# Local score stores moved from SP's DMA queue to ACT's, with a new order of phases

## The chip, the cores and the metric

The kernel runs on one core of a Trainium2 chip. The metric is the device time of one execution in microseconds. The core has a matrix engine (PE, with its weight loads shown as PEld), a vector engine (DVE), a scalar engine (ACT), a third elementwise engine (POOL) and a queue engine (SP) that here does nothing but begin DMAs. [...] DMAs are begun by SP and by ACT.

## The reference

The input is x of 8 sequences, 1024 positions, 256 channels, float32. Three residual layers follow each other:

```python
x = x + 0.5 * ffn(layernorm(x))
x = x + attn(layernorm(x))
x = x + 0.5 * ffn(layernorm(x))
```

`ffn` mixes each row with the row before it (`mu * x + (1 - mu) * x_prev`, once for k and once for r) and gives `sigmoid(xr @ W_r.T) * (relu(xk @ W_k.T)**2 @ W_v.T)`. `attn` has 16 heads of 16 channels, and looks at 40 fixed distances instead of all positions: 0 to 32, and 48, 64, 96, 128, 192, 256, 384.

```python
for i, o in enumerate(OFFSETS):
    qk = jnp.einsum('bhnd,bhnd->bhn', q, _shift(k, o))
    lg = qk * inv * (1.0 + qs[..., i]) + pos_bias[i][None, :, None]
p = jax.nn.softmax(jnp.stack(logits, axis=-1), axis=-1)
out = sum(p[..., i][..., None] * _shift(v, o))
```

Here `qs` is the product of q with a small table per distance. The result is scaled by head, multiplied by a sigmoid gate of x, and projected.

## The kernel before

Positions are handled in 32 chunks of 256 (4 a sequence) and, in the attention, in 64 tiles of 128. Groups of 512 positions (i, 16 of them, four tiles each) share the projected q. The work is written as generators, and each `yield` ends a phase:

- `ffn(c, "a")` and `ffn(c, "b")` (L230): the two FFNs of a chunk, called f1 and f2 in the plan. Normalisation: stats on DVE (L207), a chain of eight small POOL operations (L212 to L219), two scalings xn on ACT (L224), transposes on PE (L226). Then the mixing on ACT and DVE (L241, L246), three matrix products (p, L195), relu, square, tanh on ACT, the residual add on POOL (L280).
- `project(c)` (L286), p in the plan: the same normalisation, then q, k, gate and v; q to the tile qst (L311), k spread to kst (L317), v to the tile vn and from there to a DRAM buffer vd (L351).
- `scores` (L356): products of q with k for 32 rows at a time into two PSUM tiles, and two ACT copies (L370). It is called by `far` (L376) and `local` (L400).
- `local(tt)`: the scores of a tile against its own neighbourhood, copied by ACT into the SBUF tile sl (two buffers) and written by four DMAs into a DRAM buffer sl_d. A skewed address in the later read turns the band into columns by distance. `far` does the same for the long distances with sf.
- `attend(tt)` (L417): loads the logits lg from sl_d and sf_d (L425, L429); loads v (vw and v3, L435 to L446); the small product gp (L454) and its use (L458); the bias on POOL (L461); maximum and subtraction on DVE (L464, L465); exp on ACT (L467) and right behind it, on ACT's own DMA queue, the store of the near probabilities to DRAM (pd<-lg, L468); products with v for the long distances on POOL and DVE; the load of the skewed probabilities back (pd<-pd, L497); transposes (tra, L514), copies ptt on ACT (L520), products with v (pv, L527); division on DVE; on every second tile the output product (L561) and the residual add (L563).

The order is set by hand. Every phase of every generator has a place in the tables PLAN and WARP: a number of chunks, to which the chunk's or half the tile's number is added. All phases are sorted by place and emitted in that order, and every engine's queue follows it. A place is no time. With the step of one chunk the same pattern returns, with variants for even and odd tiles and for `far`, which comes twice in the first group of a sequence half and four times in the second. WARP shifts the first four and the last ten chunks.

In the program as built, the DMAs of SP and ACT together are given eight semaphores in turn. A DMA whose semaphore is still held by an earlier one waits for that one's landing, on the engine that begins it.

Of the kernel before, what the change touches and what calls it, by code (L numbers as in the profile page):

```python
# [42 lines left out]


PLAN = {
    "setup": (94.301, 95.430, 96.861),
    "f1": (-6.891, -5.181, -4.113, -3.628, -3.556, -3.503, -3.223, -3.134, -3.030, -2.933, -2.814, -2.771),
    "p": (-2.636, -2.595, -2.382, -2.366, -2.209, -2.155, -2.084, -1.868, -1.644, -1.528, -1.432),
    "f2": (1.626, 1.748, 1.930, 2.004, 2.060, 2.208, 2.297, 2.414, 2.553, 2.580, 2.713, 4.437),
    "far": (  # L50
        (-0.987, -0.918),
        (-0.874, -0.608),
        (-0.990, -0.939),
        (-0.777, -0.772),
        (-0.751, -0.627),
        (-0.528, -0.523),
    ),
    "loc": (
        (-1.515, -1.348),
        (-0.848, -0.610),  # L60
        (-1.298, -1.048),
        (-1.496, -1.489),
    ),
    "att": (
        (-0.277, -0.025, -0.020, 0.011, 0.092, 0.296, 0.358, 0.413, 0.416, 0.471, 0.743, 0.779, 0.784, 0.838, 0.892, 0.971, 1.094, 13.222),
        (-0.404, 0.000, 0.016, 0.041, 0.111, 0.194, 0.295, 0.315, 0.427, 0.447, 0.621, 0.660, 0.673, 0.723, 0.824, 0.884, 0.938, 1.093),
    ),
}
WARP = {
    ("att", 0): 0.012, ("att", 1): 0.014, ("att", 2): 0.002, ("att", 3): -0.006, ("att", 22): 0.010, ("att", 23): 0.002, ("att", 24): -0.008, ("att", 25): 0.032, ("att", 26): 0.048, ("att", 27): 0.036, ("att", 28): 0.026, ("att", 29): -0.049, ("att", 30): -0.064, ("att", 31): -0.076,  # L70
    ("f1", 0): -1.203, ("f1", 1): -0.910, ("f1", 2): -0.739, ("f1", 3): 0.153, ("f1", 22): 0.006, ("f1", 23): 0.025, ("f1", 24): -0.009, ("f1", 25): -0.004, ("f1", 26): 0.009, ("f1", 27): 0.026, ("f1", 28): 0.017, ("f1", 29): 0.027, ("f1", 30): 0.045, ("f1", 31): 0.053,
    ("f2", 0): 0.006, ("f2", 1): 0.006, ("f2", 2): -0.013, ("f2", 3): 0.001, ("f2", 22): 0.006, ("f2", 23): -0.003, ("f2", 24): 0.043, ("f2", 25): 0.041, ("f2", 26): 0.025, ("f2", 27): 0.477, ("f2", 28): 0.422, ("f2", 29): 0.543, ("f2", 30): 0.373, ("f2", 31): 0.119,
    ("far", 0): -0.275, ("far", 2): -0.001, ("far", 22): 0.004, ("far", 24): 0.035, ("far", 26): 0.044, ("far", 28): 0.047, ("far", 30): -0.024,
    ("loc", 0): -0.699, ("loc", 1): -0.010, ("loc", 2): 0.023, ("loc", 3): 0.047, ("loc", 22): 0.037, ("loc", 23): 0.007, ("loc", 24): 0.043, ("loc", 25): 0.074, ("loc", 26): 0.045, ("loc", 27): 0.056, ("loc", 28): 0.007, ("loc", 29): 0.037, ("loc", 30): 0.014, ("loc", 31): 0.120,
    ("p", 0): -0.906, ("p", 1): -0.868, ("p", 2): -0.096, ("p", 3): 0.024, ("p", 22): -0.017, ("p", 23): -0.005, ("p", 24): 0.014, ("p", 25): 0.005, ("p", 26): -0.008, ("p", 27): -0.040, ("p", 28): 0.034, ("p", 29): 0.045, ("p", 30): 0.006, ("p", 31): -0.018,
}


def flat(t, off, *dims):
    return bass.AP(tensor=t.tensor, offset=off, ap=[list(d) for d in dims])  # L80
# [3 lines left out]
def macaron(ctx: ExitStack, tc: tile.TileContext, x, wffn, watt, wo, cols, rows, pbias, se, mask, out):  # L84
    nc = tc.nc
# [270 lines left out]
    def scores(o, i, q4, keys):  # L356


        p = [ps.tile([128, 512], F32, name="p", tag=f"psq{r}", bufs=2) for r in range(2)]
        for g in range(2):  # L360
            for s in range(len(q4(0))):
                for a in range(4):
                    ms = q4(a)[s]
                    for r in range(2):
                        rows = slice(64 * r, 64 * r + 64)
                        kk = ks[g][rows, keys(ms)].rearrange("n j (h q) -> n j h q", h=2)
                        pp = p[r][32 * a : 32 * a + 32].rearrange("n (j h g q) -> n j h g q", h=2, g=2, q=2)
                        mm(pp[:, s * 32 : s * 32 + kk.shape[1], :, g], qs[i][rows, g, ms], kk, True, True)
        for r in range(2):
            nc.scalar.mul(  # L370
                o.rearrange("n j h g q -> n (j h g) q")[:, :, 2 * r : 2 * r + 2],
                p[r].rearrange("n (m q) -> n m q", q=2),
                WS**-2,
            )
# [25 lines left out]
    def local(tt):  # L400
        i, t = tt // 4, tt % 4
        sl = psb.tile([128, 64, 2, 2, 4], F32, name="sl")
        scores(
            sl,
            i,
            lambda a: [slice(t * 128 + 32 * a, t * 128 + 32 * a + 32)],
            lambda ms: slice(512 * (i % 2) + ms.start, 512 * (i % 2) + ms.start + 64),
        )
        yield
        for a in range(4):  # L410
            nc.sync.dma_start(
                flat(sl_d[i % 2], (4 * t + a) * BLK, (ROW, 32), (1, ROW)),
                sl[32 * a : 32 * a + 32].rearrange("n j h g q -> n (j h g q)"),
            )
        yield
# [165 lines left out]
    for tt in range(B * NT):  # L581
        add("loc", tt / 2, local(tt), PLAN["loc"][tt % 4])
        add("att", tt / 2, attend(tt), PLAN["att"][tt % 2])
# [66 lines left out]
```

## Time and profile before

| what | value |
|---|---|
| median of 3 runs | 1022.88 us (1022.44 to 1028.41) |
| profiled execution | 1026.83 us, of which the span from first to last instruction 1024.8 us |
| mean granted PE clock | 0.971 |
| ACT, largest groups | xn L224 104.9 us; xm L241 100.4; ptt L520 74.7; sl L370 72.7; sf L370 55.0 |
| idle time of ACT ahead of xh L291, gt L329 | 58.7 and 56.0 us, ended by PE |
| DMA | 208.75 MB, mean 204 GB/s, engines about 70% to 80% busy in the middle |
| issues by SP of sl<-sl | 256 of 128 KB, median 3.4 us to landing |
| issues by ACT of pd<-lg | 64 of 264 KB, median 2.8 us to landing |
| SP's waits for pd<-lg ahead of L497 | 203.2 us in 61 waits |

How to read it: busy time of an engine does not count instructions that only begin DMAs, nor waits. "L195 p<-kst,qst" is PE at line 195 writing p from kst and qst; a matrix product of float32 operands appears as two records. "A <- B" in the waits means that A's engine stood idle until B ended. In the timelines the columns are the start, the time, the engine (SPq, ACTq: a queue's issue of a DMA), line, operation, tiles, and in brackets the idle time before it.

### The profile page before, as it was taken

The numbers are of one execution on the slowest core, as the hardware profiler recorded it, in microseconds if no ns is written. First come the engines' busy times: TensorE is split into PE (matmuls) and PEld (weight loads), VectorE is DVE, ScalarE is ACT, GpSimd is POOL, SyncE is SP. The second block draws the span as 40 slices with busy tenths as digits, with TensorE's granted clock in tenths as the row PEclk, the third lists the DMA queues.
The fourth block names the chain that finished last, engine by engine and source line by source line (L and its number), as shares of the span: only waits on it lengthen the run. The fifth ranks groups of instructions, "written<-read, shape, count | busy, mean of one in ns | idle before, by whom it ended". The sixth has DMA issues, their size and how long they took to land.

```text
span 1024.8 us, 36078 instructions
## 1 busy us (share of the span) xinstructions
PE 951.4 (93%) x14592; PEld 781.3 (76%) x14592; DVE 831.9 (81%) x1670; ACT 610.4 (60%) x1218; POOL 695.5 (68%) x1240
## 2 busy tenths in 40 slices
PE   3888899999999999999999999999999999976775
PEld 2666688888888888888888888888888888854554
DVE  4446889988999789888999789988999789866761
ACT  3454666676666766676666766676666766543332
POOL 5434778767877688667787678767886778543641
PEclk9899999999999999999999999999999999988888
DMA  8257777768777776777877777688776777757530
GB/s 241 62 157 204 221 227 200 222 200 249 214 219 216 215 237 198 214 228 218 236 207 225 220 237 211 196 236 244 222 212 210 205 227 216 211 161 234 166 110 21
DMA packets 204365, 208.75 MB, mean 204 GB/s; under 512 B 77288, under 2 KB 162472, under 8 KB 204200
## 3 DMA queue, kind: packets, MB, share of 16 engines
q1 hardware_dynamic: 194984, 189.16, 64.8%
q10 hardware_dynamic: 9216, 17.31, 4.6%
q8 instruction: 114, 1.87, 0.8%
q14 instruction: 51, 0.42, 0.1%
HBM read 110.26 MB, written 96.14 MB: 201 GB/s over the span
## 4 chain that ended last, share of the span: by engine, by line
PE 81%; DMA 4%; POOL 4%; DVE 4%; issue 3%; ACT 2%; SPq 1%; ACTq 0%; POOLq 0%; DVEq 0%
PE p L195 55%; PE pv L195 6%; PE tra L195 5%; PE tra L514 5%; PE tr L226 5%; PE gp L195 4%; PE tra L547 1%; DMA lg<-sl 1%; ACT xn L224 1%; POOL y L213 1%; POOL x L280 1%; DMA sf<-sf 1%; DVE prod L505 1%; DMA pd<-pd 1%; DVE st L207 1%
## 5 line engine op out<-in xcount | busy, mean ns | idle before, releaser
L195 PE MATMUL p<-w_f,xm 128*128 128x256 f32 x1024 | 251.3, 389 | 0.0
L195 PEld LDWEIGHTS p<-w_f,xm 128*128 128x128 f32 x1024 | 187.5, 192 | 42.2 <-issue 12.7
L461 POOL TENSOR_TENSOR lg<-lg,bias 128x640 f32<-128x640 f32 x64 | 99.0, 1547 | 85.8 <-DVE lg L458 74.6
L195 PE MATMUL p<-xm,w_f 128*128 128x256 f32 x512 | 128.6, 396 | 8.4 <-DVE xm L248 5.2
L224 ACT ACTIVATE xn<-x,nb,y 128x256 f32<-128x256 f32 x192 | 104.9, 599 | 32.4 <-POOL nb L219 16.4
L241 ACT ACTIVATE xm<-tr,col 128x256 f32<-128x256 f32 x256 | 100.4, 475 | 39.8 <-PE tr L226 33.9
L195 PE MATMUL p<-kst,qst 64*32 64x256 f32 (+1 forms) x4096 | 123.6, 362 | 0.5 <-DVE kst L317 0.3
L246 DVE SCALAR_TENSOR_TENSOR xm<-tr,rest,xm 128x255 f32<-128x255 f32 x256 | 105.5, 474 | 21.2 <-ACT xm L241 19.9
L195 PEld LDWEIGHTS p<-xm,w_f 128*128 128x128 f32 x512 | 96.5, 198 | 25.6 <-issue 10.4
L508 POOL TENSOR_TENSOR far<-prod 128x272 f32<-128x272 f32 x64 | 49.0, 765 | 93.3 <-DVE prod L505 86.2
L280 POOL TENSOR_TENSOR x<-x,xm 128x512 f32<-128x512 f32 x64 | 81.9, 1279 | 39.9 <-DVE xm L278 39.9
L195 PE MATMUL p<-xh,wa_hi 128*128 128x256 f16 x384 | 105.1, 274 | 0.0
L195 PE MATMUL p<-xh,wa_lo 128*128 128x256 f16 x384 | 104.9, 273 | 0.0
L195 PE MATMUL p<-xl,wa_hi 128*128 128x256 f16 x384 | 104.9, 273 | 0.0
L482 POOL TENSOR_TENSOR prod<-vn,lg 128x272 f32<-128x272 f32 x144 | 94.9, 671 | 14.2 <-ACT lg L467 12.8
L520 ACT COPY ptt<-tra 128x512 f32<-128x512 f32 x128 | 74.7, 584 | 43.7 <-PE tra L514 27.8
L226 PE MATMUL tr<-ident,xn 128*128 128x128 f32 x384 | 66.4, 293 | 33.2 <-ACT xn L224 32.7
L505 DVE TENSOR_TENSOR prod<-prod 128x544 f32<-128x544 f32 (+2 forms) x120 | 93.6, 780 | 3.6
L195 PEld LDWEIGHTS pv<-vw,ptt 128*32 128x32 f32 x4096 | 69.2, 157 | 33.3 <-ACT ptt L520 17.3
L195 PEld LDWEIGHTS p<-kst,qst 64*32 64x32 f32 x4096 | 75.7, 122 | 22.9 <-issue 10.7
L317 DVE SCALAR_TENSOR_TENSOR kst<-p,col,kown 128x1024 f32<-128x1024 f32 x64 | 78.7, 1271 | 13.5 <-PE p L195 13.5
L514 PE MATMUL tra<-ident,pd 128*128 128x128 f32 x512 | 80.1, 280 | 10.3 <-DMA pd<-pd 6.7
(79 smaller groups left out, 2051.5 us busy)
## 6 DMA issues: line engine op xcount, KB each, us to landing
sl<-sl SPq DMA_DIRECT2D x256, 128.0 KB, 3.4
pd<-pd SPq DMA_DIRECT2D x64, 512.0 KB, 4.3
sf<-sf SPq DMA_DIRECT2D x184, 128.0 KB, 3.2
vw<-vd SPq DMA_DIRECT2D x128, 136.0 KB, 4.1
v<-vd SPq DMA_DIRECT2D x64, 272.0 KB, 4.4
lg<-sl SPq DMA_DIRECT2D x64, 264.0 KB, 3.9
pd<-lg ACTq DMA_DIRECT2D x64, 264.0 KB, 2.8
vd<-vn SPq DMA_DIRECT2D x32, 272.0 KB, 4.8
```

Source lines behind the costliest of these rows:

```text
L195: nc.tensor.matmul(o, l, r, start=start, stop=stop)
L224: nc.scalar.activation(xn, x2[:, i], AF.Identity, bias=nb[:, i : i + 1], scale=y[:, i : i + 1])
L226: nc.tensor.transpose(tr[:, c, i * 128 : i * 128 + 128], xn[:, c * 128 : c * 128 + 128], ident)
L241: nc.scalar.activation(xm[:, o, h], tr[:, h], AF.Identity, scale=mu[:, h : h + 1])
L246: nc.vector.scalar_tensor_tensor(x_[:, 1:256], tr[:, h, 0:255], m, x_[:, 1:256], ALU.mult, ALU.add)
L280: nc.gpsimd.tensor_tensor(x2, x2, xr, ALU.add)
L317: nc.vector.scalar_tensor_tensor(ks[g][:, o : o + 256], p[:, g].unsqueeze(2).to_broadcast([128, 256, 4]), b_k[:, g : g + 1], kown.unsqueez ...
L461: nc.gpsimd.tensor_tensor(la, la, bias[:, min(t, 3)].rearrange("p u e -> p (u e)"), ALU.add)
L482: nc.gpsimd.tensor_tensor(prod[:, k], shifted[k][1](), lf[:, k].unsqueeze(2).to_broadcast([128, 16, 17]), ALU.mult,)
L505: nc.vector.tensor_tensor(terms[:, 0:m], terms[:, 0:m], terms[:, n - m : n], ALU.add)
L514: nc.tensor.transpose(tr[:, pr * 128 : pr * 128 + 128], pd.rearrange("p (m e) -> p m e", e=8)[:, :, 4 * g + pr], ident,)
L520: nc.scalar.copy(ptt.rearrange("p q n -> p (q n)"), tr)
```

## The change

Two edits. The first is in `local`: the `yield` between the copies and the stores goes, so that both are one phase, and ACT begins the four stores instead of SP. Line numbers from there on fall by one (L468 becomes L467, L497 becomes L496).

The second is a new plan: all places in PLAN and WARP have other numbers. Most of the steady pattern keeps its order on each engine, with small moves. The lines that matter here:

```diff
 PLAN = {
...
-    "p": (-2.636, -2.595, -2.382, -2.366, -2.209, -2.155, -2.084, -1.868, -1.644, -1.528, -1.432),
+    "p": (-2.546, -2.486, -2.309, -2.298, -2.183, -2.139, -2.042, -1.760, -1.580, -1.487, -0.264,),
...
     "loc": (
-        (-1.515, -1.348),
-        (-0.848, -0.610),
-        (-1.298, -1.048),
-        (-1.496, -1.489),
+        (-1.451,),
+        (-0.919,),
+        (-1.267,),
+        (-1.435,),
     ),
     "att": (
-        (-0.277, -0.025, -0.020, 0.011, 0.092, 0.296, 0.358, 0.413, 0.416, 0.471, 0.743, 0.779, 0.784, 0.838, 0.892, 0.971, 1.094, 13.222),
-        (-0.404, 0.000, 0.016, 0.041, 0.111, 0.194, 0.295, 0.315, 0.427, 0.447, 0.621, 0.660, 0.673, 0.723, 0.824, 0.884, 0.938, 1.093),
+        (-0.069, 0.034, 0.038, 0.061, 0.197, 0.297, 0.376, 0.466, 0.481, 0.483, 0.541, 0.619, 0.797, 0.877, 0.956, 1.010, 1.189, 14.063,),
+        (-0.518, -0.024, 0.059, 0.074, 0.108, 0.255, 0.313, 0.442, 0.499, 0.501, 0.708, 0.757, 0.786, 0.836, 0.908, 0.996, 1.042, 1.175,),
     ),
 }
 WARP = {
...
-    ("f2", 0): 0.006, ("f2", 1): 0.006, ("f2", 2): -0.013, ("f2", 3): 0.001, ("f2", 22): 0.006, ("f2", 23): -0.003, ("f2", 24): 0.043, ("f2", 25): 0.041, ("f2", 26): 0.025, ("f2", 27): 0.477, ("f2", 28): 0.422, ("f2", 29): 0.543, ("f2", 30): 0.373, ("f2", 31): 0.119,
+    ("f2", 0): -0.004, ("f2", 1): -0.012, ("f2", 2): -0.026, ("f2", 3): -0.009, ("f2", 22): -0.024, ("f2", 23): -0.012, ("f2", 24): -0.009, ("f2", 25): -0.018, ("f2", 26): -0.029, ("f2", 27): 0.619, ("f2", 28): 0.412, ("f2", 29): 0.219, ("f2", 30): 0.050, ("f2", 31): 3.965,
...
 }
...
@@ def local(tt) @@
             lambda a: [slice(t * 128 + 32 * a, t * 128 + 32 * a + 32)],
             lambda ms: slice(512 * (i % 2) + ms.start, 512 * (i % 2) + ms.start + 64),
         )
-        yield
         for a in range(4):
-            nc.sync.dma_start(
+            nc.scalar.dma_start(
                 flat(sl_d[i % 2], (4 * t + a) * BLK, (ROW, 32), (1, ROW)),
                 sl[32 * a : 32 * a + 32].rearrange("n j h g q -> n (j h g q)"),
             )
```

In the order that follows from it, the steady state differs on SP and ACT more than on PE. The four stores of sl stand on ACT between the copies of a tile and whatever ACT does next. On SP the loads of vw and v3 for an odd tile now stand just ahead of the even tile's pd load, instead of behind it; the store of vd of a chunk is issued more than a chunk later; the two tiles' lg loads stand closer together. At the end, the second FFN of chunk 30 (its products, L262 to L276) comes ahead of the output product of the last tile, and the first products of that of chunk 29 ahead of the last tile's maximum. At the start, the stats of chunks 1 and 2 and the POOL chain of chunk 1 come ahead of the clearing of buffers.

## The prediction

> **What bounds the kernel now.** I read the page first, then the table of stretches, the waits, the chain that ended last, and last the timelines of single engines. The page:
>
> ```profile
> PE 951.4 (93%) x14592; PEld 781.3 (76%) x14592; DVE 831.9 (81%) x1670; ACT 610.4 (60%) x1218; POOL 695.5 (68%) x1240
> ...
> PE   3888899999999999999999999999999999976775
> ```
>
> PE is the bound, and not evenly. In the table of stretches (columns: stretch, its length, busy time of PE, PEld, DVE, ACT and POOL, granted clock, DMA share, GB/s):
>
> ```profile
> 25.00:50.00 25.00, 19.87 (x141) 14.97 (x142) 11.25 (x30) 11.25 (x23) 12.56 (x28) 0.82 0.20 56
> 500.00:600.00 100.00, 100.00 (x1676) 83.81 (x1676) 89.17 (x179) 66.19 (x135) 74.69 (x132) 1.00 0.77 220
> 925.00:950.00 25.00, 15.53 (x275) 11.23 (x281) 13.01 (x25) 8.90 (x17) 11.66 (x18) 0.77 0.76 229
> ```
>
> From 100 to 900 us PE is busy 793.9 of 800, at full clock. The other 67 us of its idle time lie before 100 (28) and after 900 (39). So in the middle, 78% of the span, a new plan has 6 us to win; whatever delays PE there is lost one for one.
>
> What can delay it? The waits name ACT; the third line is a wait of ACT for a *load that SP began*:
>
> ```profile
> PE tr L226 <- ACT xn L224: 32.7, 9, 8.9
> PE pv L195 <- ACT ptt L520: 12.6, 9, 4.0
> ACT ptt L520 <- DMA lg<-sl: 4.4, 3, 2.4
> ```
>
> A ptt copy (L520) reads no such load. The chain of waits and the timelines of ACT and PE show what happens, at 406 to 415 us:
>
> ```profile
> 406.19 7.00 DMA lg<-sl
> ```
> ```profile
> 410.53 0.74 ACT L467 ACTIVATE lg<-lg 128x640 f32<-128x640 f32 x1
> 413.27 0.33 ACTq L468 DMA_DIRECT2D pd<-lg  x1
> 413.63 0.58 ACT L520 COPY ptt<-tra 128x512 f32<-128x512 f32 x1 [2.37 <-PE p L195]
> ```
> ```profile
> 414.27 1.21 PE L195 MATMUL pv<-vw,ptt 128*32 128x34 f32 x64 [1.02 <-ACT ptt L520]
> ```
>
> The exp ends at 411.27; the store behind it, the one DMA that ACT begins now, starts at 413.27, 0.08 after that load landed at 413.19. In the built program the DMAs of SP and ACT share eight semaphores in turn, so DMA n waits until DMA n-8 has landed, whichever queue began it. Of ACT's 64 stores 15 start late in the trace, 16.2 us in all, the longest 4.40 at 927.5, each 0.07 or 0.08 us after the landing of the DMA eight before, where that is recorded. ACT's next instructions stand behind. Of four PE gaps over 1 us between 100 and 900 (2.36, 1.10, 1.02 and 1.08), the 1.10 (at 125.6) and the 1.02 follow such a late store.
>
> **The change, part by part.**
>
> *Removed from SP:* 256 stores of sl at about 0.44 us (four in 1.76 us), 113 us of its queue. SP's long wait is L497 for the landing of pd<-lg, 203 us in 61 waits, which stays. The loads that were queued behind sl may start up to 1.8 us sooner; the middle has nothing to win by it. Value 0; between -6 and 0.
>
> *Added to ACT:* 256 issues. The row is pd<-lg on ACT's queue: 0.326 us each, about 0.37 from start to start; 85 to 95 us, 1.5 a tile. ACT is 65% busy in the middle, so the cover is its slack. Behind each group of four stand: for tiles t=0 and t=1 (t is the tile's number modulo 4) the two xn of a projection, whose transposes PE runs next; for t=2 a relu and a ptt; for t=3 the gate's tanh and a ptt. Two copies end 1.3 after the last score product, four issues end at 3.0, xn at 3.6; PE has 4.4 us of other work in front of the transpose for t=0 (gp, four second-layer products, the output product) and 3.8 for t=1 (no gp). For t=2 the ptt ends at 4.2 and is due at 5.1, for t=3 the tanh's input comes only at 3.5. (Due times: mean starts of PE's matmuls in the trace of before, summed over the changed order.) Covered, by 0.2 us at the thinnest: cost 0, were nothing waited for.
>
> *The wait that is added:* each of these 256 also waits for its DMA n-8. In the changed program about 190 of them look at SP's queue. For t=0 (12 of 16 tiles) they are, in order, a v load, the pd load, an lg<-sl load, an lg<-sf load; for t=1 the pd load and a vd store are among the four; for t=2 mostly ACT's own stores, long landed; for t=3 a pd store, the pd load, two vw loads. The pd load cannot begin before the pd store has landed, and that store is ACT's own, 12 to 15 of ACT's instructions earlier. So ACT waits for a round trip that it started itself. The pieces:
>
> ```profile
> pd<-pd SPq DMA_DIRECT2D x64, 512.0 KB, 4.3
> ...
> lg<-sl SPq DMA_DIRECT2D x64, 264.0 KB, 3.9
> ...
> vd<-vn SPq DMA_DIRECT2D x32, 272.0 KB, 4.8
> ```
> ```profile
> 599.10 0.33 ACTq L468 DMA_DIRECT2D pd<-lg  x1
> ...
> 603.43 1.19 ACT L370 ACTIVATE sl<-p 128x512 f32<-128x512 f32 x2
> ```
> ```profile
> 602.64 0.53 SPq L497 DMA_DIRECT2D pd<-pd  x1
> ```
> ```profile
> 607.19 0.60 PE L226 MATMUL tr<-ident,xn 128*128 128x128 f32 x4
> ```
>
> These are a t=0 tile of before. Work it with the changed order: pd store 599.10; pd load 602.64 (3.5 later); it lands at 606.9 by its 4.3. Behind it SP issues vd, lg<-sl (at 603.7, lands 607.6) and lg<-sf (second at 604.7, lands by its 3.2 us at 607.9). ACT's copies end at 604.62, but its second store starts at 607.0, its fourth at 607.9, and ACT is free at 608.3. xn ends at 608.9; PE wanted it at 607.19. Stall 1.7 us; with median latencies 1.5. Bounds: 0 (a fast pd store, 2.0 us instead of 3.5) and 3.5 (at 367.9 this store took 5.4).
>
> For t=1 in the first half of a pair the last of the four waits for the vd store right behind the pd load: 3.5 + 0.6 + 4.8 = 8.9 after the pd store, ACT free at 9.3, xn at 9.9; due 7.5 to 8.3 (PE's cover is 0.6 less, but the exp may come up to 0.8 earlier): 1.6 to 2.4. In the second half four sf stores stand between (2.2 to 2.8 us more on SP), against some 2.5 us more PE and ACT work before the scores: about the same, up to 4.7. I take 2.0; bounds 0.3 and 4.7. For t=2 and t=3 0; up to 1.
>
> Sum: leaving out the first and last tiles, 14 x 1.5 + 14 x 2.0 = 49 us; bounds 4 and 115. Stalls of 3.4 us or more would also cost clock: PE gaps of 3.48, 3.60 and 4.74 us (at 61, 83 and 904) are each followed by 3.4 to 6.8 us at half clock, those of 2.36 and less are not; nothing for the value, up to 20 us at the high end.
>
> [...]
>
> *The plan, middle:* PE's groups come in nearly the same order; by the mean starts of before the changed order of all matmuls sums to 2 us less, which I take as 0.
>
> *The plan, ends:* at the start the stats of chunks 1 and 2 come before the clearing of buffers, but PE's gap of 6.4 us at 20.4 waits for chunk 0's residual, stats and xn, which stay: 0, between -5 and +5. At the end chunk 30's second FFN moves ahead of the last tile's output product, and chunk 29's mixing on DVE (1.65 us), now right ahead of the last tile's maximum, comes earlier. Now chunk 31's L241 waits 1.7 us, until 1007.3, for chunk 30's add on POOL: -3, between -8 and +4, for ACT's new stores sit there too.
>
> Sum: the profiled execution took 1026.8 with a span of 1024.8; +49 - 3 gives 1072.8. It is 4 us above the median of the three runs, 1022.9, so the forecast is **1068**.
>
> **Rivals.** *The waits are covered:* SP without its stores runs ahead, the round trip shortens by 1.5 us or ACT's exp comes earlier, and a stall of 0 to 0.5 remains on some 28 tiles: 1023 to 1035, say 1027. For it: PE's gaps after late stores are few in before, and 0.6 to 0.8 us late cost nothing. Against it: the round trip is 7.8 us, the copies end 5.5 after its start.
>
> *Faster:* the one mechanism is the tail. After 900 us PE idles 39 of 125 us, the clock falls to 0.77, and if chunks 27 to 30 fill these gaps, up to a third of the idle time and the half clock behind it goes: 15 us, 1008 to 1018. It decides only if the stalls of the middle stay under 5 us in all, 0.2 a tile.
>
> *Worse:* stalls over 3.4 us on the second halves, the clock halved behind them: 1095 to 1140.
>
> **How the numbers follow.** Forecast 0.58, covered 0.24, faster 0.08, worse 0.10. A change under 1%, 10 us, I count as none. Faster than 1012.6: most of the third case, 0.05. Slower than 1033.1: the first, the last and a sixth of the covered case, 0.72. The rest is 0.23. The range 1022 to 1105 leaves out the faster case, a part of the covered one and half of the worse. Given the forecast alone I would say 1040 to 1095.
>
> **What would show it.** Right: in the middle PE shows gaps of 1 to 3 us before the tr of L226, released by ACT xn; ACT's waits name DMAs (pd<-pd, vd<-vn, lg<-sf) ahead of xn; stores of sl on ACT's queue with 2 to 4 us between copy and last issue; PE's share falls to about 89%. Wrong: PE still at 99% in the middle, or gaps before other matmuls (pv, p), or ACT's stores 0.37 us apart throughout.

## The result, and the profile after

The changed kernel takes 1231.21 us, the median of three runs (1226.09 to 1231.45), against 1022.88. The ratio on record is 1.2007, with a 95% interval of 1.1951 to 1.2063. It is slower, as forecast, but by 208 us where 45 were forecast, and above the range. The profiled execution has a span of 1223.8 us; before it was 1024.8.

The page of the changed kernel, with the busy times and the slices:

```profile
PE 1015.9 (83%) x14592; PEld 804.5 (66%) x14592; DVE 851.3 (70%) x1670; ACT 616.8 (50%) x1218; POOL 676.3 (55%) x1240
...
PE   3868788898798889988888988988899998877774
...
PEclk9888899999999999999899988999999998989878
```

PE does the same 14592 instructions but is busy 65 us longer, and the row of nines is gone. The table of stretches (length; busy time of PE, PEld, DVE, ACT and POOL; granted clock; DMA share; GB/s) for the three stretches shown of before:

```profile
25.00:50.00 25.00, 17.22 (x92) 12.97 (x93) 13.43 (x36) 9.66 (x21) 12.75 (x32) 0.82 0.19 55
...
500.00:600.00 100.00, 83.57 (x1260) 66.44 (x1259) 70.59 (x143) 52.47 (x105) 55.87 (x102) 0.95 0.66 185
925.00:950.00 25.00, 24.40 (x377) 20.14 (x375) 22.77 (x45) 16.11 (x34) 16.73 (x29) 1.00 0.64 187
```

The middle has lost both ways: PE stands 16 of 100 us, and its clock is no longer 1.00. (At 925 us this kernel is still in its middle.) The waits (engine that waits, for whom; us in total, times, longest):

```profile
PE tr L226 <- ACT xn L224: 156.6, 36, 8.8
...
ACT xn L224 <- DMA sl<-sl: 106.8, 18, 7.7
```

The first was 32.7 us before; the second is new. One tile t=0 shows what happens. ACT, SP and PE in the timeline:

```profile
511.69 0.34 ACTq L467 DMA_DIRECT2D pd<-lg  x1
...
516.29 1.18 ACT L370 ACTIVATE sl<-p 128x512 f32<-128x512 f32 x2
518.37 6.29 ACTq L410 DMA_DIRECT2D sl<-sl  x4
524.72 1.09 ACT L224 ACTIVATE xn<-x,nb,y 128x256 f32<-128x256 f32 x2 [7.24 <-DMA sl<-sl]
```
```profile
512.96 2.05 SPq L434 DMA_DIRECT2D vw<-vd  x2
515.10 0.56 SPq L440 DMA_DIRECT2D v<-vd  x1
515.71 0.46 SPq L444 DMA_DIRECT2D v<-vd  x1
516.26 0.53 SPq L496 DMA_DIRECT2D pd<-pd  x1
516.84 0.58 SPq L351 DMA_DIRECT2D vd<-vn  x1
517.52 0.42 SPq L424 DMA_DIRECT2D lg<-sl  x1
517.98 3.10 SPq L428 DMA_DIRECT2D lg<-sf  x3
```
```profile
518.32 1.89 PE L195 MATMUL tra<-wot,yt 128*128 128x256 f32 x8
525.37 1.18 PE L226 MATMUL tr<-ident,xn 128*128 128x128 f32 x4 [5.16 <-ACT xn L224]
```

The copies end at 517.47. The four stores need 0.31 us each, but the last begins at 524.36, and xn, ACT's next instruction, starts 0.36 us behind that and 7.2 us after the copies. Put beside the DMA that stands eight places earlier in the built program:

```
store begins   the DMA eight before   begun    landed
518.37         v<-vd    (SP)          515.10   518.30
522.15         pd<-pd   (SP)          516.26   522.13
523.61         lg<-sl   (SP)          517.52   523.59
524.36         lg<-sf   (SP)          519.50   524.34
```

Each store begins 0.02 to 0.07 us after that landing, and in the trace each carries the same semaphore as the DMA beside it. PE had work until 520.21 and then stood 5.16 us. Between 150 and 900 us there are 21 such stalls ahead of the transposes, one for each chunk, 93.5 us in all: 4.87 us on average for t=0 (11 of them), 3.15 and 4.84 for t=1 in the first and second half of a pair (5 each). For t=2 the four stores look mostly at ACT's own old stores: one such tile has its copies end at 492.91 and the stores begin at 492.94, 493.29, 493.76 and 494.24, and PE has no gap behind it.

The whole difference can be put in two terms. Let the half-clock time be the time with a granted clock of 0.5 in the clock records, and count half of it as lost. Then span = PE idle + half of the half-clock time + a rest, and the rest hardly moves between these two kernels (in the other runs it lies between 910 and 940 us):

| kernel | span | PE idle | at half clock | rest |
|---|---|---|---|---|
| before | 1024.8 | 73.4 | 59.0 | 921.9 |
| changed | 1223.8 | 207.9 | 186.2 | 922.8 |

So 134.5 of the 199 us are PE standing and 63.6 are PE at half clock behind a stall. Between 100 and 900 us, before had no half-clock time at all and the changed kernel 99.0 us.

By place: the k spread of chunk 4 (kst, L317) starts at 123.5 us before and at 150.4 after, that of chunk 31 at 897.3 and 1093.1, and the end takes 127.5 and 130.7 us more. The start costs 27 us, the middle 169 (6.3 us for each of 27 chunks), the end 3.

### The profile page after: what moved, and what is told of

Read it like the earlier page. It is cut to its first block, busy times and chain, and to the rows that moved or that the text cites. A ratio compares the mean times of both kernels' runs of the same rounds, so it can differ in the third digit from the quotient of the medians.

```text
span 1223.8 us, 36053 instructions
## 1 busy us (share of the span) xinstructions
PE 1015.9 (83%) x14592; PEld 804.5 (66%) x14592; DVE 851.3 (70%) x1670; ACT 616.8 (50%) x1218; POOL 676.3 (55%) x1240
## 3 DMA queue, kind: packets, MB, share of 16 engines
q10 hardware_dynamic: 21504, 50.88, 12.7%
## 4 chain that ended last, share of the span: by engine, by line
PE 50%; DMA 18%; POOL 10%; ACT 6%; DVE 5%; SPq 5%; issue 4%; ACTq 1%; POOLq 0%; DVEq 0%
PE p L195 36%; PE pv L195 4%; DMA lg<-sf 4%; PE tra L513 4%; PE tr L226 4%; POOL prod L481 4%; DMA sl<-sl 3%; DMA vd<-vn 3%; DMA pd<-pd 2%; ACT xn L224 2%; PE gp L195 2%; DMA sf<-sf 2%; DVE prod L504 2%; DMA v<-vd 2%; POOL x L280 1%
## 5 line engine op out<-in xcount | busy, mean ns | idle before, releaser
L226 PE MATMUL tr<-ident,xn 128*128 128x128 f32 x384 | 77.6, 325 | 157.5 <-ACT xn L224 156.6
L460 POOL TENSOR_TENSOR lg<-lg,bias 128x640 f32<-128x640 f32 x64 | 99.0, 1546 | 127.5 <-DVE lg L457 113.3
L226 PEld LDWEIGHTS tr<-ident,xn 128*128 128x128 f32 x384 | 45.3, 156 | 181.5 <-ACT xn L224 179.4
L195 PE MATMUL p<-xm,w_f 128*128 128x256 f32 x512 | 156.7, 461 | 5.8 <-DVE xm L248 3.6
L481 POOL TENSOR_TENSOR prod<-vn,lg 128x272 f32<-128x272 f32 x144 | 117.0, 824 | 47.4 <-ACT lg L466 44.7
L195 PE MATMUL p<-kst,qst 64*32 64x256 f32 (+1 forms) x4096 | 136.6, 381 | 2.1 <-issue 1.6
L195 PEld LDWEIGHTS p<-xm,w_f 128*128 128x128 f32 x512 | 117.0, 240 | 32.1 <-issue 4.9
L292 DVE TENSOR_TENSOR xl<-tr,xh 128x512 f16<-128x512 f32 x32 | 22.1, 692 | 137.8 <-ACT xh L291 137.8
L317 DVE SCALAR_TENSOR_TENSOR kst<-p,col,kown 128x1024 f32<-128x1024 f32 x64 | 79.2, 1280 | 51.5 <-PE p L195 51.5
L212 POOL TENSOR_SCALAR va<-mv 128x2 f32<-128x2 f32 x96 | 33.1, 345 | 130.7 <-DVE mv L208 125.3
L504 DVE TENSOR_TENSOR prod<-prod 128x544 f32<-128x544 f32 (+2 forms) x120 | 99.4, 828 | 7.5 <-POOL prod L481 2.3
L513 PE MATMUL tra<-ident,pd 128*128 128x128 f32 x512 | 84.8, 291 | 18.5 <-ACT ptt L519 12.9
```

The source lines that it names most:

```text
L195: nc.tensor.matmul(o, l, r, start=start, stop=stop)
L226: nc.tensor.transpose(tr[:, c, i * 128 : i * 128 + 128], xn[:, c * 128 : c * 128 + 128], ident)
L317: nc.vector.scalar_tensor_tensor(ks[g][:, o : o + 256], p[:, g].unsqueeze(2).to_broadcast([128, 256, 4]), b_k[:, g : g + 1], kown.unsqueez ...
L460: nc.gpsimd.tensor_tensor(la, la, bias[:, min(t, 3)].rearrange("p u e -> p (u e)"), ALU.add)
L481: nc.gpsimd.tensor_tensor(prod[:, k], shifted[k][1](), lf[:, k].unsqueeze(2).to_broadcast([128, 16, 17]), ALU.mult,)
L504: nc.vector.tensor_tensor(terms[:, 0:m], terms[:, 0:m], terms[:, n - m : n], ALU.add)
```

## The experiments

Theory: ACT's stores stand until the DMA eight places before has landed, mostly one of SP's, and xn stands behind them. Rivals: the new order of phases by itself; the time of ACT's issues; and within the theory, two accounts of why SP's DMAs are late: the round trip from ACT's own pd store over the pd load (the forecast's account), or anything that SP's queue stands for.

### The queue alone, the phase alone, the plan alone

Four kernels: the changed one with SP's stores; the kernel before with ACT's stores in one phase; the same in its two phases; and the kernel before with SP's stores in one phase.

```diff
-            nc.scalar.dma_start(
+            nc.sync.dma_start(
```

> The changed kernel with its new plan and its single phase, but the four stores begun by SP again. Shared semaphores (the stores on ACT's queue stand until SP's DMA eight before has landed, and xn stands behind them): the whole loss goes, PE has no gaps over 1 us before the transposes of L226 except perhaps two or three, 1010 to 1035 us. The new order of phases: the loss stays, over 1150 us. If it comes out under 1018, the new plan is worth something by itself, most likely at the end.

The next three start from the kernel before. In the two that drop the `yield`, "loc" keeps the first place of each pair.

```diff
-        yield
         for a in range(4):
-            nc.sync.dma_start(
+            nc.scalar.dma_start(
```

> The kernel before, its old plan kept, with the four stores begun by ACT right behind its copies (the second phase is dropped). Shared semaphores: in the built program a tile t=0 now waits in turn for the pd load, a vw load, a v load and a vd store, t=1 for a vw load, two v loads and a vd store, so both classes stall and the time is 1130 to 1280 us. The new order of phases: the order is the old one, so no more than 1040 us. Issue time of ACT: the same 256 issues as in the changed kernel, so about 1230 us as there, but with ACT's issues 0.37 us apart and no wait between them.

```diff
         yield
         for a in range(4):
-            nc.sync.dma_start(
+            nc.scalar.dma_start(
```

> The kernel before, its old plan and its two phases, with only the queue of the four stores changed from SP to ACT. Shared semaphores: the stores of t=0 stand behind xh, those of t=1 some 14 us behind the pd store, so most of what they look at has landed; 1023 to 1065 us. Issue time of ACT: 256 issues as in the changed kernel, so about 1200 us. Any DMA on ACT's queue that shares semaphores with SP costs as much wherever it stands: about 1200 us too.

```diff
-        yield
         for a in range(4):
             nc.sync.dma_start(
```

> The kernel before with its old plan and SP's stores, but all in one phase: the four stores directly behind the copies in the order of the program. If SP's waits for the copies make the loss of the new plan with SP's stores, it shows here too: 1035 to 1060 us. If the places of the other phases make it: 1020 to 1032 us.

| plan, phases of the stores | begun by SP | begun by ACT |
|---|---|---|
| before, two | 1022.88 | 1116.12, ratio 1.0902 (1.0864 to 1.0940) |
| before, one | 1035.67, 1.0108 (1.0077 to 1.0139) | 1231.42, 1.2019 (1.1955 to 1.2083) |
| new, one | 1056.79, 1.0314 (1.0277 to 1.0350) | 1231.21, 1.2007 (1.1951 to 1.2063) |

In one phase the queue costs 174 us with the new plan and 196 with the old one; it needs no new plan to be slow. With SP's stores the changed kernel is 22 us above the expected range, but its middle is nearly whole again; a stretch of it:

```profile
500.00:600.00 100.00, 99.13 (x1584) 81.01 (x1579) 89.25 (x175) 65.63 (x130) 73.76 (x130) 1.00 0.76 215
```

So the new plan costs something by itself, 3.1%, which the forecast had at -3 us. And ACT's stores cost 93 us even at their old place, twice the 42 that the expectation allowed at most. There t=0's stores stand behind xh, and t=1's, ahead of the two xn, are never late between 100 and 900 us. The loss is at t=3, whose stores are late by 41 us in all, of 50 for all of ACT's DMAs; behind them stand the gate's tanh and a ptt copy, and PE waits for that copy:

```profile
ACT gt L329 <- DMA sl<-sl: 59.2, 11, 6.6
PE tra L514 <- ACT ptt L520: 46.6, 18, 4.5
```

The waits of the kernel before with ACT's stores in one phase:

```profile
PE tr L226 <- ACT xn L224: 94.4, 24, 8.8
ACT xn L224 <- DMA sl<-sl: 93.3, 16, 8.3
PE tra L513 <- ACT ptt L519: 84.9, 32, 6.4
```

Here the old plan puts the copies and stores of t=2, and then a ptt copy, behind the late stores of t=1, and PE's wait goes with them: about half of it is now at the transposes tra, for a ptt copy of ACT.

### Only half of the tiles

```diff
-            nc.scalar.dma_start(
+            (nc.sync if t < 2 else nc.scalar).dma_start(
```

> The changed kernel with the stores of the tiles t=0 and t=1 begun by SP again and those of t=2 and t=3 left to ACT. Shared semaphores: ACT no longer stands ahead of the xn of a projection, 1010 to 1040 us, although half of the issues on ACT stay. Issue time of ACT: half the loss stays, about 1125 us. The new order of phases: over 1150 us.

Measured 1095.7 us, ratio 1.0697 (1.0646 to 1.0748): not as expected. The large stalls ahead of L226 are gone, but 39 us are lost against SP's stores alone. The stores of t=2 did no harm in the changed kernel, where they looked mostly at ACT's own stores. With those of t=0 and t=1 on SP, the DMA eight before is an lg load for all four stores in ten of the 16 tiles t=2, and the stores of t=2 stand 35 us in all between 100 and 900 us (those of t=3, which look at the same DMAs as before, 6). The waits show it at the transposes tra:

```profile
PE tra L513 <- ACT ptt L519: 39.6, 23, 5.1
```

What a store looks at depends on every DMA of both queues between it and the eighth before it.

### One store for four

```diff
-        for a in range(4):
-            nc.scalar.dma_start(
-                flat(sl_d[i % 2], (4 * t + a) * BLK, (ROW, 32), (1, ROW)),
-                sl[32 * a : 32 * a + 32].rearrange("n j h g q -> n (j h g q)"),
-            )
+        nc.scalar.dma_start(
+            flat(sl_d[i % 2], 4 * t * BLK, (BLK, 4), (ROW, 32), (1, ROW)),
+            sl.rearrange("n j h g q -> n (j h g q)"),
+        )
```

> The changed kernel with one store of four blocks for each tile where there were four, still begun by ACT right behind its copy. Shared semaphores: the only store now looks at a v load for t=0 and for t=1 in the first half of a pair, which has landed or lands within 1 us, and at the pd load for t=1 in the second half, which still costs some 2 us on 8 tiles with half clock behind; 1030 to 1065 us. Issue time of ACT: three quarters of it goes, so a quarter of the loss stays, about 1075 us, spread over all tiles. The new order of phases: over 1150 us.

Measured 1272.98, ratio 1.2446 (1.2389 to 1.2504): slower than all, and no verdict on the theory, since the edit brought a cost of its own. ACT and SP in the timeline:

```profile
503.51 0.53 ACTq L409 DMA_DIRECT2D sl<-sl  x1
...
505.93 0.32 ACTq L466 DMA_DIRECT2D pd<-lg  x1
...
515.66 0.53 ACTq L409 DMA_DIRECT2D sl<-sl  x1
```
```profile
515.66 0.53 SPq L495 DMA_DIRECT2D pd<-pd  x1
```

The pd load waits for the landing of the pd store, which stands behind the large store, and begins 9.7 us after it; for the tiles t=3 the median of that time is 8.3 us, and 2.1 in the changed kernel. In the packet records of ACT's queue the store of 512 KB has mostly four packets of 4 KB in flight and never more than six, and its last packet ends 9.8 us after the issue (median; 8.2 to 13.4); the four stores of 128 KB have 16 and more in flight at their peak, and the last packet of one ends 2.1 us after its issue (median). Why the store of four blocks keeps so few in flight, no run here shows.

### Behind xn instead of ahead of it

```diff
     "loc": (
-        (-1.451,),
-        (-0.919,),
-        (-1.267,),
-        (-1.435,),
+        (-1.451, -1.29),
+        (-0.919, -0.79),
+        (-1.267, -1.266),
+        (-1.435, -1.434),
...
+        yield
         for a in range(4):
             nc.scalar.dma_start(
```

> The changed kernel with the same stores on ACT's queue, but for t=0 and t=1 begun in a phase of their own that is placed behind the two xn and the xh of the projection. Shared semaphores: the stores still stand until DMAs of SP have landed, two to four of them late, but the transposes of L226 no longer stand behind them, and PE has some 5 us of work by then; the stall falls from about 4.4 us to under 1 us a chunk: 1060 to 1100 us, near the 1057 of the same plan with SP's stores. Issue time of ACT: the issues are the same in number, so about 1230 us.

Measured 1111.46, ratio 1.0857 (1.0827 to 1.0887). With the same 256 issues, 120 us of the 174 are gone: what stands behind the stores makes the price, not the issues. The time is 11 us above the expected range; in the waits what is left is at a ptt copy, most often the one behind the stores of t=2 (the first line is no more than with SP's stores, where it is 43.7):

```profile
PE tr L226 <- ACT xn L224: 44.0, 12, 9.1
PE tra L514 <- ACT ptt L520: 36.7, 30, 2.8
```

### Which of SP's DMAs

Three edits of the changed kernel: the pd load begun by POOL; the pd load ahead of the vw and v loads on SP's queue, as before; and the pd load by POOL together with more buffers, so that SP's loads of vw and v3 need not wait for PE and POOL.

```diff
-        nc.sync.dma_start(pd, flat(pd_d, 4 * t4 * BLK, (ROW, 32), (BLK, 4), (1, ROW)))
+        nc.gpsimd.dma_start(pd, flat(pd_d, 4 * t4 * BLK, (ROW, 32), (BLK, 4), (1, ROW)))
```

> The changed kernel with the pd load alone moved from SP's queue to POOL's, all else kept: SP no longer stands until ACT's pd store has landed, and the pd load is not among the DMAs that share semaphores. Shared semaphores, with the round trip that ACT starts itself: the lg loads and the vd store land 1 to 4 us sooner, the stalls of 4.4 us before the transposes fall to 0 to 2.5 us and the half clock behind them mostly goes: 1070 to 1140 us, unless POOL, which now stands for the pd store, becomes late itself. If the stall came from ACT's issues or from the new order of phases, it stays at about 1230 us.

```diff
     "att": (
...
-        (-0.518, -0.024, 0.059, 0.074, 0.108, 0.255, 0.313, 0.442, 0.499, 0.501, 0.708, 0.757, 0.786, 0.836, 0.908, 0.996, 1.042, 1.175,),
+        (-0.518, -0.010, 0.059, 0.074, 0.108, 0.255, 0.313, 0.442, 0.499, 0.501, 0.708, 0.757, 0.786, 0.836, 0.908, 0.996, 1.042, 1.175,),
```

> The changed kernel with one place of its plan moved by 0.014, so that on SP's queue the pd load stands ahead of the vw and v loads again, as before; PE's order is the same. If the swap made the excess of the stall, t=0 falls from 4.9 to some 2 us and half of the half clock goes: 1130 to 1180 us. If the stores, which now look at a vw load, a v load, the vd store and an lg load, find these as late as they found the pd load, the time stays at 1200 to 1240 us.

```diff
-    vw = [const.tile([128, 4, 2, 8, 17], F32, name=f"vw{i}") for i in range(2)]
+    vw = [const.tile([128, 4, 2, 8, 17], F32, name=f"vw{i}") for i in range(4)]
...
-        lazy["pv1"] = pool("pv1", 2)
+        lazy["pv1"] = pool("pv1", 3)
...
-        vwt = vw[tt % 2]
+        vwt = vw[tt % 4]
...
-        nc.sync.dma_start(pd, flat(pd_d, 4 * t4 * BLK, (ROW, 32), (BLK, 4), (1, ROW)))
+        nc.gpsimd.dma_start(pd, flat(pd_d, 4 * t4 * BLK, (ROW, 32), (BLK, 4), (1, ROW)))
```

> The changed kernel with three waits of SP taken away: the pd load goes to POOL's queue, the vw tile gets four buffers for two (no wait for PE's pv), the v3 tile three for two (no wait for POOL's products). ACT's stores, their phase and the plan stay. With the pd load alone moved the time stayed at 1225, and SP then stood 371 us at the vw loads for PE. If ACT's stores are late because SP's DMAs, in order, stand for other engines before they start, SP now runs ahead, what the stores look at has landed, and the stalls before the transposes of L226 fall under 1.5 us: 1055 to 1120 us. If SP's DMAs are late for their own length (3 to 6 us each with eight at most in flight over both queues), the stalls stay over 2.5 us: 1150 to 1240 us.

The first two gave 1224.6 (1.1971, 1.1929 to 1.2014) and 1229.1 (1.1995, 1.1957 to 1.2034): no gain. Both speak against the round trip. With the pd load on POOL, SP's own waits in the trace are

```profile
SPq L434 <- PE tr L226: 245.0, 25, 13.5
SPq L434 <- PE pv L195: 126.0, 36, 18.5
```

SP stands no less, only for something else: the vw loads wait until PE has used the tile's buffer. And the kernel with the pd load ahead, in a tile t=0, SP and ACT in the timeline:

```profile
731.70 0.53 SPq L496 DMA_DIRECT2D pd<-pd  x1
732.28 1.26 SPq L434 DMA_DIRECT2D vw<-vd  x2
733.64 0.54 SPq L440 DMA_DIRECT2D v<-vd  x1
...
734.74 0.43 SPq L351 DMA_DIRECT2D vd<-vn  x1
735.21 0.47 SPq L424 DMA_DIRECT2D lg<-sl  x1
735.72 2.83 SPq L428 DMA_DIRECT2D lg<-sf  x3
```
```profile
729.42 0.34 ACTq L467 DMA_DIRECT2D pd<-lg  x1
...
734.37 1.17 ACT L370 ACTIVATE sl<-p 128x512 f32<-128x512 f32 x2
737.85 3.48 ACTq L410 DMA_DIRECT2D sl<-sl  x4
741.38 1.09 ACT L224 ACTIVATE xn<-x,nb,y 128x256 f32<-128x256 f32 x2 [5.83 <-DMA sl<-sl]
```

The pd load now starts 2.28 us after its store (that is also the median for these tiles; 4.07 in the changed kernel). Yet ACT is free 5.8 us after the copies here, and 7.13 on average over 11 tiles t=0, where it was 6.91. The stores look at other DMAs: the vw load begun at 732.28 (landed 737.78), the v load at 733.64, the vd store at 734.74 and the first lg<-sf at 735.72, which landed at 741.00, 0.02 us ahead of the fourth store. The four start in the 3.3 us up to the end of the copies or behind it, and the two whose landing is recorded land over 5 us later.

The third gave 1182.2 (1.1506, 1.1460 to 1.1551), in the upper of its two expected ranges, but what it was to decide went two ways. For t=0 no store is late any more between 100 and 900 us, and ACT is free 2.1 us after the copies (6.6 with the pd load alone on POOL). But the stores of t=1, t=2 and t=3 now stand 21, 26 and 18 us in all, and SP did not run ahead; its longest waits are now

```profile
SPq L397 <- ACT sf L370: 340.9, 40, 39.8
SPq L424 <- DMA sl<-sl: 144.3, 62, 6.8
```

where they were 77.4 and 34.1 us in the changed kernel. So for t=0 it was SP's waits for other engines that made the stores late. How much of the rest comes from such waits and how much from the DMAs' own 3 to 6 us, with at most eight in flight over both queues, this run does not separate.

That the wait is for the eighth DMA before is shown across kernels whose stores look at different DMAs. Counted between 100 and 900 us: ACT's DMAs that begin over 0.3 us after ACT's instruction before, the sum of these delays, and how many begin within 0.12 us after the landing of the eighth before, of those where the landing is recorded.

| kernel | ACT's DMAs | late | us | at that landing |
|---|---|---|---|---|
| changed, SP's stores | 55 | 1 | 0.4 | 1 of 1 |
| before | 56 | 14 | 12.7 | 12 of 12 |
| stores behind xh | 256 | 36 | 41.2 | 32 of 32 |
| ACT for t=2, t=3 | 156 | 23 | 42.8 | 13 of 13 |
| before, ACT, two phases | 254 | 37 | 49.9 | 26 of 28 |
| pd by POOL, more buffers | 240 | 62 | 80.1 | 43 of 43 |
| pd by POOL | 225 | 51 | 93.9 | 40 of 41 |
| before, ACT, one phase | 221 | 83 | 95.7 | 61 of 61 |
| pd load ahead | 221 | 72 | 108.9 | 32 of 32 |
| changed | 225 | 76 | 110.0 | 69 of 69 |

In all 329 of 332, half of them within 0.03 us. In the traces of before and of the changed kernel the 1205 DMAs of SP and ACT carry the same eight semaphores, and of the 1047 whose predecessor on the semaphore has its landing recorded none begins before that landing, in either trace. No run took the wait itself away on the same queue.

### A third queue

```diff
-            nc.scalar.dma_start(
+            nc.gpsimd.dma_start(
```

> The changed kernel with its four stores begun by POOL right behind ACT's copies: in the built program these wait only for POOL's own stores eight before, two tiles back, and not for a DMA of SP. Shared semaphores: ACT stands for nothing, and PE's stalls of 4.4 us before the transposes go; what is left is POOL, which now stands until ACT's copies end and then issues four times, 2 to 2.4 us a tile on an engine that is busy 10.6 of some 16 us a tile: 1060 to 1150 us. If it is not the semaphores but the store traffic in this phase that delays PE, the time stays at about 1230 us.

Measured 1206.13, ratio 1.1765 (1.1726 to 1.1805), above the range. The waits:

```profile
ACT xn L224 <- POOL nb L219: 160.8, 52, 10.5
PE tr L226 <- ACT xn L224: 140.8, 47, 10.1
POOL sl L410 <- ACT sl L370: 105.3, 38, 13.2
```

ACT no longer stands for a DMA, but POOL stands 105 us for ACT's copies and then issues for 2 us, and behind it are the eight small operations that give xn its factors. The same PE wait comes by another way: here, too, an engine with work on the path begins a store whose data comes late. So this run does not isolate the shared semaphores.

### Where the new plan loses

With SP's stores the new plan is 10.7 us later at chunk 4, 15.3 more at chunk 31, and 1 at the end. Three suspects: the shifts of the first chunks, SP standing for the copies in the one phase (95 us in all in that kernel, 9.5 before), and the vw loads ahead of the pd load.

Three kernels start from the changed one with SP's stores. The first takes the set-up phases and WARP for chunks and tiles 0 to 3 from before; the second gives the stores their second phase back, as far behind the copies as before; the third has the move of 0.014 shown above.

```diff
-    "setup": (95.086, 95.678, 97.065,),
+    "setup": (94.301, 95.430, 96.861),
```
```diff
-        (-1.451,),
-        (-0.919,),
-        (-1.267,),
-        (-1.435,),
+        (-1.451, -1.284),
+        (-0.919, -0.681),
+        (-1.267, -1.017),
+        (-1.435, -1.428),
...
+        yield
         for a in range(4):
```

> The changed kernel with the stores begun by SP, and with the set-up phases and the shifts of the first four chunks and tiles taken from the plan of before. With SP's stores the new plan was about 11 us later at chunk 4, 15 us more by chunk 31, and even at the end. If the start's loss comes from these shifts, chunk 4 comes 8 to 11 us sooner and the time is 1045 to 1050 us; if it comes from the general places, nothing changes, 1057 us.

> The changed kernel with the stores begun by SP and put into a second phase again, as far behind the copies as the plan of before put them. With the same new plan, but in one phase, SP stood 95 us for ACT's copies and the time was 1057 us. If those waits, with SP's loads behind them, make the loss of the new plan, it goes here: 1018 to 1035 us. If the new places of the other phases make it, it stays: 1048 to 1062 us.

> The changed kernel with SP's stores and the same swap undone. If the swap makes the loss of the new plan: 1020 to 1038 us. If not: 1048 to 1064 us.

Measured 1056.77 (1.0337, 1.0311 to 1.0362), 1061.65 (1.0353, 1.0323 to 1.0382) and 1055.71 (1.0291, 1.0257 to 1.0324), against 1056.79. None of the three is the cause. In the first, chunk 4 comes 1.6 us sooner, where 8 to 11 were expected if the shifts were it. The one phase costs 11 us in the old plan (1.0108), just inside the range expected of a cause, and nothing that could be seen in the new one. By the sum used above, the 26.9 us that the new plan with SP's stores adds to the span are 13.1 of PE idle, 5.4 of half clock and 8.4 in the rest. What in the new places costs them stays open. No kernel of the series beats the one before.

## Why the forecast was right in kind and wrong in size

**The bound.** Right: PE had nothing to spare in the middle, and 169 of the 199 us of span were lost there.

**ACT's issues: cost 0.** Right as far as it can be seen: the tiles t=2 issue four stores in 1.7 us without a gap of PE behind them.

**The added wait.** Right in kind, place and order: the gaps are ahead of the transposes of L226, released by xn, on t=0 and t=1 and not on t=2 and t=3, and the four DMAs looked at are those named. This is the term of the sum that was mis-sized, and the largest: of the 208 us, 174 go with the queue and 34 with the new plan. For t=0, PE's cover was right: 2.6 us after the copies in the forecast, 2.74 in the tile above. But ACT was to be free 3.7 us after the copies and was free after 6.9; the difference, 3.2, added to the forecast's 1.7 gives the 4.9 measured.

The step that failed is "Work it with the changed order", which took the pieces from a tile of before: the pd load 3.5 after its store, landing 4.3 later, the last lg load about 1 us behind. In the changed kernel they are 4.08 and 5.88 on average, and 2.2 in the tile above. There four loads of vw and v stand ahead of the pd load on SP's queue, a swap that was listed in the change and not carried into the sum. With the swap undone the first two fall to 2.85 and 4.13, but the stall stays, because the stores then look at other DMAs that are as late: so the swap explains the sizes of these pieces, and would not by itself have given the right stall. For t=1 the forecast had 2.0, and the changed kernel shows 3.15 and 4.84. Carried over to the forecast's 28 tiles, an estimate, that is 14 x 4.87 + 14 x 4.0 = 124 us, not 49, and beyond the upper bound of 115.

**The round trip.** The forecast said that "ACT waits for a round trip that it started itself". That is too narrow. With the pd load moved to POOL, or started 2 us sooner, the stores look at other DMAs of SP and are about as late. It is the newest DMAs of SP that the shared order puts eight places ahead, and for t=0 they were late because SP, in order, stood for other engines; the pd store is one of several things that it stands for.

**The clock.** Taken as 0, with 20 us at the high end; it was 63.6. It followed from the first error: 20 of the 21 stalls, 4.5 us on average, have half clock behind them, and the gaps in the middle of before, 2.36 us at most, had none. The forecast counted stalls of 3.4 us or more. That was too high a bound: in the changed kernel a stall of 2.48 was followed by 3.41 us at half clock (one of 2.91 by none), and the kernel before already had a gap of 3.20 us, at 40.8, with 3.41 us at half clock behind it.

**The plan.** Middle 0, start 0 and end -3 were taken; with SP's stores they are +15, +11 and +1, for a reason that stays open. That PE's changed order sums to 2 us less by the mean starts of before says nothing of how the other engines meet that order.

**The rivals.** "Worse" had the right mechanism, stalls over 3.4 us with half clock behind, but on the second halves alone, and at 0.10. "Faster" rested on the tail, which gained nothing. "Covered" wanted stalls of 0.5 us at most.

## What to carry to other kernels

Where two queues draw in turn on one set of semaphores, as SP and ACT on the eight here, a DMA on a compute engine's queue can wait for a transfer of the other queue that it has nothing to do with: 329 of ACT's 332 late DMAs above began at the landing of the DMA eight before. Before moving one, list for each which DMA stands that many places ahead in the new program, when it starts there, and what stands behind the waiting instruction. Take the durations from transfers with the same company in flight, not from a median, and price a stall of PE at its length plus half of the clock stretch that may follow: here stalls from 2.48 us on had 3.41 or 6.83 us at half clock behind them, 20 of 21. A store whose data comes late did least harm here on the engine that has nothing else to do: 1056.79 us on SP, 1206.13 on POOL, 1231.21 on ACT.

## What was not expected of the hardware

The half clock comes in steps. Between 100 and 900 us of the changed kernel there are 17 stretches of 3.41 us and 6 of 6.83, and no other lengths; 20 of the 21 stalls, from 2.48 to 5.71 us, are followed by one. A stall of 2.48 us was enough, and one of 2.91 was not. Over all sixteen traces, between 120 and 900 us, each of the 98 PE gaps of 3.41 us or more has a half-clock stretch that begins in it or within 3.5 us behind it, and so have 39 of the 53 gaps from 2.4 to 3.41 us and 1 of the 47 from 1.0 to 1.5.

The one store of four blocks took some 10 us for 512 KB (9.8 at the median), and the pd load that waits for the store behind it on its queue began late: 8.3 us after that store for the tiles t=3, where it was 2.1.
